# A graph attention kernel on one core: the first block of adj in two transfers, fewer and larger stores, one more small load

## The chip, the cores and the metric

The kernel runs on one core of one Trainium2 chip. The metric is device time in microseconds (us): the median of three runs. The profile is one further execution on the chip, taken by the hardware profiler. Engine names are those of the profile: PE is the matrix engine, PEld its weight load, DVE the vector engine, ACT the scalar engine, POOL GpSimd, SP the engine that here only issues transfers. A small q after a name (SPq) means its sequencer, which waits and issues.

## The reference

One graph attention layer with four heads, a residual and a layer norm. Cut to what matters:

```python
# x: 4096 x 512, adj: 4096 x 4096, W: 512 x 2048, a: 4 x 1024 x 1, all float32
ht  = (x @ W).reshape(N, 4, 512).transpose(1, 0, 2)
src = einsum('hnd,hd->hn', ht, a[:, :512, 0])
dst = einsum('hnd,hd->hn', ht, a[:, 512:, 0])
e   = leaky_relu(src[:, :, None] + dst[:, None, :], 0.01) + adj[None]
h   = einsum('hij,hjd->hid', softmax(e, axis=-1), ht).mean(axis=0)
out = layernorm(x + h)          # over the last axis, eps 1e-5
```

The inputs of adj are mostly zero, with entries up to 1e9 and a diagonal that is not zero. Where the largest entry of a row of adj is far enough ahead of the second, the softmax of that row is one at that column and zero elsewhere.

## The kernel before

The kernel uses that. It finds the column of the largest entry of each row of adj, gathers that row of x, and multiplies it by the mean of the four heads' parts of W; then come the residual and the layer norm. Beside it, it works out a bound on what src and dst can add, and counts the rows in which the lead of the largest entry is too small. If there were any, a general branch (`general`) would do those blocks in full; it is not taken here.

The 4096 rows are 32 blocks of 128, one row on each of the 128 partitions: block `ib` has rows `p * 32 + ib`. A block of adj is 128 x 4096 numbers, 2 MB, and a row of it 16 KB, contiguous in memory. The whole program is written in order by hand (`manual_schedule`), engine by engine.

`leading_rows` does the work. Its loads and its stores are issued on SP, those of `a` on ACT, the gathers on POOL:

- `load_adj` (L124) loads one block of adj into one of six buffers. Blocks 28 to 30 come in two pieces, block 31 in four. `load_x` (L127) and `load_w` (L130) load several blocks of x, or half of W, into one large tile `hold`.
- At the start SP issues adj of block 0, half of W, adj of block 1, the other half of W, adj of blocks 2 to 4, x of blocks 0 to 3. ACT issues the four transfers of `a` (L135), two rows of 2 KB each, into `a_rows`.
- In the loop over blocks `t`, SP loads adj of block `t + 5`. DVE reduces block `t` to maxima of segments (L180), finds the best segment (L187, L189), and POOL gathers that segment (L200). Two blocks behind, DVE finds the column in it (L217, L223) and POOL gathers the row of x (L211). Three blocks behind, PE turns that row (L238), adds x (L246) and multiplies by `w_sum` (L253); ACT takes the statistics (L275, L277) and writes the results over x in `hold` (L286).
- PE also builds `w_sum` from W (L343, from the first half of W on) and, from W and `a`, the vectors for the bound (L353, L359, L367).
- The last blocks are written out by hand after the loop. The results are stored by `store` (L338), all on SP, at the end: blocks 0 to 7 by four, 8 to 15 by two, 16 to 23 by four, then blocks 28 and 29, 24 and 25, 26 and 27, then 30, then 31.

Two kinds of waits hold SP. A transfer into a buffer of adj waits until DVE has read what was in it. And there are eight semaphores for the transfers of SP and ACT together, given out in turn in the order of the program: each transfer waits until the one eight before it has landed. There are 64 such transfers in the program. After the last, SP waits for the semaphores one by one, in a fixed order, and the program ends.

Of the kernel before, what the change touches and what calls it, by code (L numbers as in the profile page):

```python
# [9 lines left out]
F32 = mybir.dt.float32  # L10
# [10 lines left out]
P = 128  # L21
# [9 lines left out]
def gat_resnorm_kernel(  # L31
# [29 lines left out]
    any_bad = keep.tile([1, 1], I32, name="any_bad")  # L61

    leading_rows(tc, x, adj, W, a, out, ident, v, n_bad, any_bad)

    flag = nc.values_load(any_bad[0:1, 0:1], min_val=0, max_val=N)
# [5 lines left out]
def leading_rows(ctx, tc, x, adj, W, a, out, ident, v, n_bad, any_bad):  # L71
# [8 lines left out]
    nc = tc.nc  # L80
    N, D = x.shape
    H = a.shape[0]
    KB, NB = D // P, N // P
    AHEAD = 5
    Q = 4
    PIECES = 4
    LATE = NB - Q
    BEHIND = LATE - Q

    once = ctx.enter_context(tc.tile_pool(name="once", bufs=1))  # L90
    adj_pool = ctx.enter_context(tc.tile_pool(name="adj_pool", bufs=AHEAD + 1))
# [7 lines left out]
    adj_rows = adj.rearrange("(p nb) m -> nb p m", nb=NB)  # L99
# [11 lines left out]
    a_rows = once.tile([2 * H, D], F32, name="a_rows")  # L111

    once.tile([P, 32], F32, name="pad_end")
    adj_t = {}

    def pieces(ib):
        return PIECES if ib == NB - 1 else 2 if ib >= LATE else 1

    def load_adj(ib):
        if 0 <= ib < NB:  # L120
            t = adj_t[ib] = adj_pool.tile([P, N], F32, name="adj_t")
            n = pieces(ib)
            for k in range(n):
                nc.sync.dma_start(t[:, ts(k, N // n)], adj_rows[ib][:, ts(k, N // n)])  # L124
# [4 lines left out]
    def load_w(kb, n):  # L129
        nc.sync.dma_start(hold[:, ds(w_at + kb * H, n * H), :], w_blocks[:, ds(kb * H, n * H), :])  # L130

    load_adj(0)
    for s in range(2):
        for h in range(0, H, H // 2):
            nc.scalar.dma_start(  # L135
                a_rows[ds(s * H + h, H // 2), :], a[ds(h, H // 2), ts(s, D), :].rearrange("h d o -> h (d o)")
            )
    for kb in range(0, KB, 2):
        load_w(kb, 2)
        load_adj(kb // 2 + 1)  # L140
# [196 lines left out]
    def store(queue, lo, n):  # L337
        queue.dma_start(out_rows[:, ds(lo, n), :], hold[:, ds(lo, n), :])  # L338
# [93 lines left out]
    for t in range(NB):  # L432
# [29 lines left out]
        ib = t - PROJECT  # L462
# [25 lines left out]
    for ib in range(BEHIND, LATE):  # L488
        row_norm(ib)
    nc.scalar.activation(xx, xx, AF.Sqrt)  # L490
    for ib in range(0, 2 * Q, Q):
        store(nc.sync, ib, Q)
    for ib in range(2 * Q, 4 * Q, 2):
        store(nc.sync, ib, 2)
    for ib in range(4 * Q, BEHIND, Q):
        store(nc.sync, ib, Q)
    add_x(nc.gpsimd, BEHIND)
    find_column(NB - 2)
# [208 lines left out]
```

## Time and profile before

| | |
|---|---|
| three runs | 234.88, 235.20, 235.32 us; median 235.20 |
| the profiled execution | 234.9 us, of which 233.4 are the span from its first to its last instruction |
| PE, DVE, ACT, POOL busy | 199.9, 191.3, 111.8, 100.7 us |
| DMA | 12257 packets, 97.12 MB, 416 GB/s over the span |
| transfers of SP and ACT (queues q1 and q10) | 88.1 MB; 89.1% of the DMA engines' time over the span |
| gathers of POOL (queue q0) | 8.84 MB; 9.6% |
| a block of adj, from issue to landing | 30.8 us in the median |

The page divides the span into 40 slices of 5.8 us; a digit there is the busy share in tenths. "Chain" is the work that ended last, followed back from the last instruction to what released each step. In a timeline line stand the start, the time taken, the engine, the line of the kernel, the operation, the tiles written and read, and in brackets the idle time before and what ended it. In a line of busy time by stage stand the stage, its length, the busy time of PE, PEld, DVE, ACT and POOL with counts, the granted clock of PE, the DMA engines' busy share and the rate in GB/s.

### The profile page before, as it was taken

The numbers are of one execution on the slowest core, as the hardware profiler recorded it, in microseconds if no ns is written. First come the engines' busy times: TensorE is split into PE (matmuls) and PEld (weight loads), VectorE is DVE, ScalarE is ACT, GpSimd is POOL, SyncE is SP. The second block draws the span as 40 slices with busy tenths as digits, with TensorE's granted clock in tenths as the row PEclk, the third lists the DMA queues.
The fourth block names the chain that finished last, engine by engine and source line by source line (L and its number), as shares of the span: only waits on it lengthen the run. The fifth ranks groups of instructions, "written<-read, shape, count | busy, mean of one in ns | idle before, by whom it ended". The sixth has DMA issues, their size and how long they took to land.

```text
span 233.4 us, 2484 instructions
## 1 busy us (share of the span) xinstructions
PE 199.9 (86%) x683; PEld 105.3 (45%) x683; DVE 191.3 (82%) x300; ACT 111.8 (48%) x267; POOL 100.7 (43%) x215
## 2 busy tenths in 40 slices
PE   0069995999999999999999779879998977999980
PEld 0034644646565555665645244334443433444460
DVE  0548299689929999999788995999999999998881
ACT  2001223014474757575767455545664644188561
POOL 2020234414524464644543452647464564548300
PEclk9999999579999999999999979999999999999997
DMA  6999999999999999999999999999999999999995
GB/s 237 423 432 428 428 438 426 415 439 436 422 421 437 423 431 425 431 419 428 430 430 428 432 423 432 423 430 421 426 433 420 426 423 426 412 424 420 421 414 213
DMA packets 12257, 97.12 MB, mean 416 GB/s; under 512 B 1992, under 2 KB 2440, under 8 KB 6480
## 3 DMA queue, kind: packets, MB, share of 16 engines
q1 hardware_dynamic: 8640, 88.08, 89.1%
q0 software_dynamic: 3584, 8.84, 9.6%
q8 instruction: 6, 0.10, 0.2%
q14 instruction: 11, 0.09, 0.1%
q10 hardware_dynamic: 16, 0.02, 0.0%
HBM read 88.54 MB, written 8.39 MB: 415 GB/s over the span
## 4 chain that ended last, share of the span: by engine, by line
DMA 64%; DVE 21%; PE 11%; SPq 1%; issue 1%; ACT 0%; DVEq 0%
DMA adj_t<-in_adj_dram 53%; DVE seg L180 17%; DMA hold<-in_x_dram 11%; PE o L253 6%; PE o L295 2%; DVE at L189 1%; PE tp L238 1%; DVE top L187 1%; PE o L246 1%; DVE within L223 1%; SPq L130 1%; PE o L291 0%; SPq L124 0%; DVE inner L217 0%; ACT hold L335 0%
## 5 line engine op out<-in xcount | busy, mean ns | idle before, releaser
L180 DVE TENSOR_REDUCE seg<-adj_t 128x128 f32<-128x2048 f32 (+3 forms) x66 | 145.5, 2208 | 28.5 <-DMA adj_t<-in_adj_dram 28.2
L253 PE MATMUL o<-w_sum,yt 128*128 128x512 f32 x248 | 117.6, 616 | 0.7 <-ACT yt L240 0.7
L253 PEld LDWEIGHTS o<-w_sum,yt 128*128 128x128 f32 x248 | 45.6, 196 | 55.2 <-issue 43.9
L240 ACT COPY yt<-tp 128x512 f32<-128x512 f32 x32 | 18.8, 588 | 43.9 <-PE tp L238 43.8
L200 POOL DMA_INDIRECT lead<-in_adj_dram,row x32 | 32.3, 1008 | 14.6 <-POOL row L196 14.6
L211 POOL DMA_INDIRECT y<-in_x_dram,col x32 | 30.9, 964 | 15.4 <-POOL col L225 15.1
L238 PE MATMUL tp<-ident,y 128*128 128x128 f32 x128 | 22.1, 296 | 10.2 <-DMA y<-in_x_dram,col 10.1
L246 PE MATMUL o<-hold,ident 128*128 128x512 f32 x52 | 28.5, 634 | 1.7 <-DMA hold<-in_x_dram 1.7
L343 PE MATMUL o<-hold,ident 128*128 128x512 f32 x32 | 17.3, 696 | 13.6 <-DMA hold<-in_L_gnn_W_dram 13.6
L238 PEld LDWEIGHTS tp<-ident,y 128*128 128x128 f32 x128 | 18.5, 209 | 22.8 <-issue 20.5
L361 ACT COPY wt<-tp 128x512 f32<-128x512 f32 x16 | 9.2, 587 | 38.2 <-PE tp L359 38.2
L196 POOL TENSOR_TENSOR row<-at,first 128x1 uint32<-128x1 uint32 x32 | 6.1, 190 | 43.6 <-DVE at L189 43.6
L367 PEld LDWEIGHTS pv<-at_d,wt 128*128 128x128 f32 x128 | 17.2, 200 | 7.4 <-ACT wt L361 3.7
L260 ACT ACTIVATE sq<-hold 128x512 f32<-128x512 f32 x32 | 19.8, 620 | 0.0
L225 POOL TENSOR_TENSOR col<-start,within 128x1 uint32<-128x1 uint32 x31 | 5.9, 190 | 32.2 <-DVE within L223 32.2
L286 ACT ACTIVATE hold<-o,nm,sd 128x512 f32<-128x512 f32 x24 | 17.2, 771 | 0.0
L277 ACT ACTIVATE sq<-o,nm 128x512 f32<-128x512 f32 x24 | 16.5, 687 | 0.8
L343 PEld LDWEIGHTS o<-hold,ident 128*128 128x128 f32 x32 | 6.9, 225 | 21.5 <-issue 21.5
L367 PE MATMUL pv<-at_d,wt 128*128 128x2 f32 x128 | 16.0, 249 | 0.6 <-ACT wt L361 0.6
L344 ACT ACTIVATE w_sum<-o 128x512 f32<-128x512 f32 x4 | 2.4, 598 | 27.5 <-PE o L343 27.5
L275 ACT ACTIVATE sq<-o 128x512 f32<-128x512 f32 x24 | 14.5, 606 | 0.0
L187 DVE MAX8 top<-seg 128x8 f32<-128x256 f32 (+2 forms) x32 | 11.6, 362 | 1.1
(86 smaller groups left out, 140.0 us busy)
## 6 DMA issues: line engine op xcount, KB each, us to landing
adj_t<-in_adj_dram SPq DMA_DIRECT2D x28, 2048.0 KB, 30.8
adj_t<-in_adj_dram SPq DMA_DIRECT2D x6, 1024.0 KB, 28.1
hold<-in_L_gnn_W_dram SPq DMA_DIRECT2D x2, 2048.0 KB, 16.4
hold<-in_x_dram SPq DMA_DIRECT2D x2, 2048.0 KB, 37.6
out_dram<-hold SPq DMA_DIRECT2D x4, 1024.0 KB, 16.1
out_dram<-hold SPq DMA_DIRECT2D x7, 512.0 KB, 14.4
hold<-in_x_dram SPq DMA_DIRECT2D x3, 1024.0 KB
adj_t<-in_adj_dram SPq DMA_DIRECT2D x4, 512.0 KB, 19.8
```

Of the source, the lines that this page charges most:

```text
L180: nc.vector.tensor_reduce(seg_of[ib][:, ts(k, N // e // n)], adj_t[ib][:, ts(k, N // n)].rearrange("p (s e) -> p s e", e=e), axis=AX.X, op ...
L200: nc.gpsimd.indirect_dma_start(out=lead, out_offset=None, in_=adj_segs[e], in_offset=bass.IndirectOffsetOnAxis(ap=row[:, :1], axis=0),)
L211: nc.gpsimd.indirect_dma_start(out=y, out_offset=None, in_=x, in_offset=bass.IndirectOffsetOnAxis(ap=col[:, :1], axis=0),)
L238: nc.tensor.transpose(tp[:, kb, :], y[:, ds(kb, P, KB)], ident)
L240: nc.scalar.copy(yt, tp)
L246: nc.tensor.matmul(o_ps[ib], ident, hold[:, ib, :], start=start, stop=False)
L253: nc.tensor.matmul(o_ps[ib], yt_of[ib][:, kb, :], w_sum[:, kb, :], start=(start and kb == 0), stop=(kb == KB - 1),)
L260: nc.scalar.activation(sq, hold[:, ib, :], AF.Square, accum_out=xx[:, ib : ib + 1])
L277: nc.scalar.activation(sq, o, AF.Square, bias=nm[:, i], accum_out=sd[:, i])
L286: nc.scalar.activation(hold[:, ib, :], o_ps.pop(ib), AF.Identity, bias=nm[:, i], scale=sd[:, i])
L343: nc.tensor.matmul(o, ident, hold[:, w_at + kb * H + h, :], start=(h == 0), stop=(h == H - 1))
L367: nc.tensor.matmul(pv[:, kb, h : 2 * H : H], wt[:, k, :], at_d[:, k, h : 2 * H : H], start=(k == 0), stop=(k == KB - 1),)
```

## The change

Three edits in `leading_rows`:

1. Adj of block 0 is loaded in two transfers into the same buffer, partitions 0 to 15 and partitions 16 to 127.
2. The eight rows of `a` come in five transfers instead of four: 2, 2, 2, 1 and 1 rows.
3. The results of blocks 8 to 15 are stored by four blocks like their neighbours: two transfers instead of four.

```diff
-    load_adj(0)
-    for s in range(2):
-        for h in range(0, H, H // 2):
-            nc.scalar.dma_start(
-                a_rows[ds(s * H + h, H // 2), :], a[ds(h, H // 2), ts(s, D), :].rearrange("h d o -> h (d o)")
-            )
+    def load_adj_in_parts(ib, *parts):
+        t = adj_t[ib] = adj_pool.tile([P, N], F32, name="adj_t")
+        for lo, hi in zip((0, *parts), (*parts, P)):
+            nc.sync.dma_start(t[lo:hi, :], adj_rows[ib][lo:hi, :])
+
+    load_adj_in_parts(0, P // 8)
+    for s, h, n in ((0, 0, H // 2), (0, H // 2, H // 2), (1, 0, H // 2), (1, 2, 1), (1, 3, 1)):
+        nc.scalar.dma_start(a_rows[ds(s * H + h, n), :], a[ds(h, n), ts(s, D), :].rearrange("h d o -> h (d o)"))
     for kb in range(0, KB, 2):
         load_w(kb, 2)
         load_adj(kb // 2 + 1)
...
     nc.scalar.activation(xx, xx, AF.Sqrt)
-    for ib in range(0, 2 * Q, Q):
-        store(nc.sync, ib, Q)
-    for ib in range(2 * Q, 4 * Q, 2):
-        store(nc.sync, ib, 2)
-    for ib in range(4 * Q, BEHIND, Q):
+    for ib in range(0, BEHIND, Q):
         store(nc.sync, ib, Q)
```

The number of transfers of SP and ACT is 64 after the change as well: one more for adj, one more for `a`, two fewer stores. Here Q is 4, P 128, H 4 and BEHIND 24.

## The prediction

> **What bounds the kernel now.** I read the page first: which resource is never idle.
>
> ```profile
> DMA  6999999999999999999999999999999999999995
> GB/s 237 423 432 428 428 438 426 415 439 436 422 421 437 423 431 425 431 419 428 430 430 428 432 423 432 423 430 421 426 433 420 426 423 426 412 424 420 421 414 213
> DMA packets 12257, 97.12 MB, mean 416 GB/s; under 512 B 1992, under 2 KB 2440, under 8 KB 6480
> DMA 64%; DVE 21%; PE 11%; SPq 1%; issue 1%; ACT 0%; DVEq 0%
> ```
>
> The DMA row is at 9 in every slice but the first and the last, at 412 to 439 GB/s. 97.12 MB at 427 GB/s is 227.4 us of a span of 233.4. So the kernel is one stream of transfers, and about 6 us in which the stream starts and ends. The chain agrees: 64% of it is DMA. To see the two ends I asked for busy time by stage:
>
> ```profile
> 0.00:2.00 2.00, 0.00 (x0) 0.00 (x0) 0.00 (x0) 0.00 (x0) 1.06 (x10) 1.00 0.05 10
> 2.00:2.50 0.50, 0.00 (x0) 0.00 (x0) 0.00 (x0) 0.00 (x0) 0.38 (x6) 1.00 0.60 131
> 2.50:3.00 0.50, 0.00 (x0) 0.00 (x0) 0.00 (x0) 0.42 (x1) 0.00 (x0) 1.00 1.29 360
> 3.00:4.00 1.00, 0.00 (x0) 0.00 (x0) 0.00 (x0) 0.86 (x1) 0.00 (x0) 1.00 0.77 328
> 4.00:9.00 5.00, 0.00 (x0) 0.00 (x0) 0.33 (x1) 0.00 (x0) 0.00 (x0) 1.00 0.99 422
> 24.00:210.00 186.00, 172.94 (x606) 91.77 (x605) 164.61 (x245) 96.97 (x232) 90.32 (x187) 0.96 1.01 427
> 210.00:230.00 20.00, 16.62 (x59) 8.95 (x57) 15.84 (x46) 12.84 (x34) 7.20 (x11) 1.00 1.00 413
> 230.00:231.00 1.00, 0.00 (x0) 0.00 (x0) 0.00 (x0) 0.00 (x0) 0.00 (x0) 0.92 0.73 283
> 231.00:232.00 1.00, 0.00 (x0) 0.00 (x0) 0.00 (x0) 0.00 (x0) 0.00 (x0) 0.50 0.13 49
> ```
>
> The last two figures of a row are the DMA share and GB/s. Nothing flows before 2.0 us. From 2.0 to 4.0 the core moves 0.5 x 131 + 0.5 x 360 + 328 = 574 KB, where full rate gives 854: the ramp costs 280 KB, or 0.66 us. Then the timeline of the first 30 us (start, length, engine and line):
>
> ```profile
> 0.98 0.39 SPq L124 DMA_DIRECT2D adj_t<-in_adj_dram  x1
> 1.06 1.49 ACTq L135 DMA_DIRECT2D a_rows<-in_L_gnn_a_dram  x4
> 8.67 4.48 DVE L180 TENSOR_REDUCE seg<-adj_t 128x128 f32<-128x2048 f32 x2 [8.67 <-DMA adj_t<-in_adj_dram]
> 13.61 6.46 PE L343 MATMUL o<-hold,ident 128*128 128x512 f32 x8 [13.61 <-DMA hold<-in_L_gnn_W_dram]
> 18.34 4.48 DVE L180 TENSOR_REDUCE seg<-adj_t 128x128 f32<-128x2048 f32 x2 [4.20 <-DMA adj_t<-in_adj_dram]
> ```
>
> Block 0 lands at 8.67 and block 1 at 18.34, with half of W between: 4.84 us for each 2 MB. With 16 engines and 8 rows each, a 16 KB row takes 0.605 us. The issue at 0.98 to the landing is 7.69, so starting the stream costs 2.85. What is lost there is not made up: every engine has the same work and is full from there to 230. The tail shifts with it: in the chain, x of the last blocks (issued 176.29, landed 201.51) releases a run of PE work to the last DVE and ACT steps (228.77), the last store and the end.
>
> [...]
>
> **The change, part by part.** The sum is against the profiled execution, 234.9 us (span 233.4 and 1.5 around it), 0.3 under the median of 235.2.
>
> First 16 rows alone. [...]every engine is late by **+1.9**. Below: 0[...]. Above: no more than +1.9[...].
>
> The other 112 rows. [...]I take **+1.0**[...].
>
> The earlier start. A list of 16 rows may be spread over the engines sooner than one of 128. At most the ramp's 0.66 us comes back, at least nothing. The second issue follows within 0.4 us, less than a first row takes, so no engine runs dry. I take **-0.3**.
>
> SP's queue. There is one issue more at the head, 0.39 at most, which pushes W and block 1 back; the landing of rows 0 to 15 is waited for before block 1 is issued, and that of the 112 rows before the second half of W, because eight semaphores go round and each transfer waits for the one eight before. Behind the second wait stand blocks 2 to 4, x and block 5, which stood behind block 0's landing before as well. The cover is data already queued: half of W to 13.6 and block 1 to 18.3. Even a block 0 that lands at 13 leaves 5 us. **0**; without that cover the engines would stand idle until the landing. After the start each transfer waits for the same one as before.
>
> The fifth transfer of a. ACT issues once more, 0.24 to 0.54 us (those of now: 238/309/537 ns), ahead of a table load at 2.58; ACT's first operation that counts is at 20.11, and PE's first use of a at 20.0. On the DMA engines it adds one row's worth of 2 KB: under 0.1. **0**.
>
> Stores of 8 to 15. Two transfers of 1 MB take the place of four of 512 KB. Nothing is computed or waited for longer: blocks 8 to 15 were finished long before SP gets there at 202, and their two transfers wait for the first two quarters of the last block, as the first two did. Blocks 16 to 23 follow two places earlier, so they no longer wait for x; the last stores wait for earlier stores than now. [...]2 MB at the tail's 413 against 427 GB/s is 0.16 us, an estimate with 0 at the other end. **-0.15**. The count of transfers is 64 before and after, so the waits at the end keep their order.
>
> Sum: 1.9 + 1.0 - 0.3 - 0.15 = +2.45, 237.35 against 234.9, and with the 0.3 to the median **237.6**. Ends: 0 + 0 - 0.66 - 0.16 = -0.8 (234.4) and 1.9 + 2.4 - 0 - 0 = +4.3 (239.5).
>
> **Rivals.** *[...]the stream only starts sooner.* Then -0.3 - 0.15 is 234.75, at best 234.4. For it: the ramp is there to be had, and no packet of this trace shows two engines in each other's way. [...]It decides on one point: whether the first 16 rows take under about 1.0 us (0.6 and the gains of 0.45) or more. *Only the first transfer is hit*: 1.9 - 0.45 gives 236.65; for it, nothing shows how 112 rows are laid out[...]. *The 112 rows collide fully*: 239.1 to 239.5. *A wait of SP starves the stream*: for it, SP does wait for landings here; against, over 5 us of queued data; it needs block 0 at 18 us, and each us after that adds 1. *The change isn't what it says*: excluded, the built program holds the two transfers, 16x4096 and 112x4096, on SP.
>
> **How the numbers follow.** [...]in one of three degrees: 0.67, and every degree is slower by more than 0.2%, which is about what a measurement of this kernel can tell from no change (0.47 us: 234.73 to 235.67). [...]0.33. Then the forecast of -0.45 lies at the bound, its spread is 0 to -0.8: 0.21 faster and 0.12 the same. As both signs hold chance, the likeliest case alone is 236.5 to 239.5. The range of 234.4 to 239.3 adds the other case and leaves out the worst collisions and a starved stream.
>
> **What would show it.** Right: DVE's first reduction of block 0 starts at 10.5 to 12.5 instead of 8.67, the first slice of GB/s falls below 237, block 1 is reduced some 2 to 4 us after 18.34, the middle slices stay at 427, and the chain's last steps shift by the same. First transfer alone: the landing of rows 0 to 15, seen where SP issues block 1, comes near 5 us after a start at 2[...]. Wrong: block 0 reduced at 8.3 or earlier, or a later block catching up with its old time, which would mean that the stream has slack that I deny.

## The result, and the profile after

The changed kernel takes 238.18 us (median of four runs, 238.15 to 238.20) against 235.22 for the kernel before: a ratio of 1.0128, 95% interval 1.0111 to 1.0146, or 2.96 us slower. The profiled execution took 238.15 us, with a span of 236.6 (233.4 before). The forecast was 237.6, slower, in a range of 234.4 to 239.3.

The page of the changed kernel, the DMA rows and the chain:

```profile
DMA  6999999999999999999999999999999999999995
GB/s 148 295 432 425 432 433 414 437 434 421 421 427 433 432 426 422 440 417 427 429 426 433 424 431 429 425 429 422 427 433 420 422 427 425 411 426 424 423 397 219
PE 36%; DMA 22%; POOL 18%; issue 17%; DVE 2%; ACT 1%; ACTq 1%; POOLq 0%; DVEq 0%
```

The digits of the DMA row are the same as before; only the rate tells the difference. The first two slices carry 148 and 295 GB/s where they carried 237 and 423: 217 GB/s less over slices of 5.9 us is 1.28 MB, which at 427 GB/s is 3.0 us. From the third slice on the two kernels look alike. So the digit counts time in packets, not bytes: with a digit of 9 the second slice moved 295 GB/s here and 423 before. A packet can take longer: at 5 to 6 us of the stages that follow, a share of 1.15 is 18.4 us of the 16 engines for 19.2 rows of 16 KB, 0.96 us a row, against 0.61 at 4 to 9 us before (0.99 at 422 GB/s). The shares of the chain are of no use here. It runs back through PE, POOL and gathers this time and shows 22% of DMA, though 97.12 MB still fill the span.

Busy time by stage of the changed kernel (the last two figures are the DMA share and GB/s):

```profile
2.00:2.50 0.50, 0.00 (x0) 0.00 (x0) 0.00 (x0) 0.00 (x0) 0.37 (x6) 1.00 2.33 496
2.50:3.00 0.50, 0.00 (x0) 0.00 (x0) 0.00 (x0) 0.18 (x1) 0.00 (x0) 1.00 0.64 98
3.00:4.00 1.00, 0.00 (x0) 0.00 (x0) 0.00 (x0) 1.00 (x1) 0.00 (x0) 1.00 1.30 213
4.00:5.00 1.00, 0.00 (x0) 0.00 (x0) 0.00 (x0) 0.10 (x1) 0.00 (x0) 1.00 0.35 98
5.00:6.00 1.00, 0.00 (x0) 0.00 (x0) 0.00 (x0) 0.00 (x0) 0.00 (x0) 1.00 1.15 315
6.00:7.00 1.00, 0.00 (x0) 0.00 (x0) 0.00 (x0) 0.00 (x0) 0.00 (x0) 1.00 0.82 229
7.00:9.00 2.00, 0.00 (x0) 0.00 (x0) 0.00 (x0) 0.00 (x0) 0.00 (x0) 1.00 1.11 322
9.00:14.00 5.00, 0.00 (x0) 0.00 (x0) 2.01 (x1) 0.00 (x0) 0.00 (x0) 1.00 0.96 342
24.00:210.00 186.00, 173.32 (x603) 92.69 (x602) 164.40 (x241) 94.06 (x225) 88.86 (x186) 0.95 1.01 427
```

A packet is counted in the stage in which it starts, so that a DMA share (the figure before GB/s) can be above 1. From 2.0 to 2.5 the first rows start at 496 GB/s, where the kernel before had 131; the part on the prediction comes back to this. Then comes a hole down to 98 GB/s at 4 to 5 us (SP finds the 16 rows landed at 5.38), and after it 229 to 342 GB/s until 14 us. The middle is at 427 as before.

The timeline of its first 30 us:

```profile
0.97 0.86 SPq L135 DMA_DIRECT2D adj_t<-in_adj_dram  x2
...
2.50 0.35 SPq L124 DMA_DIRECT2D adj_t<-in_adj_dram  x1
...
5.38 0.33 SPq L130 DMA_DIRECT2D hold<-in_L_gnn_W_dram  x1
7.02 5.01 SPq L124 DMA_DIRECT2D adj_t<-in_adj_dram  x3
11.99 4.48 DVE L182 TENSOR_REDUCE seg<-adj_t 128x128 f32<-128x2048 f32 x2 [11.99 <-DMA adj_t<-in_adj_dram]
...
16.84 6.39 PE L345 MATMUL o<-hold,ident 128*128 128x512 f32 x8 [16.84 <-DMA hold<-in_L_gnn_W_dram]
...
21.56 4.48 DVE L182 TENSOR_REDUCE seg<-adj_t 128x128 f32<-128x2048 f32 x2 [4.10 <-DMA adj_t<-in_adj_dram]
```

Block 0 is reduced at 11.99 instead of 8.67 (+3.32), W is used at 16.84 instead of 13.61 (+3.23), block 1 is reduced at 21.56 instead of 18.34 (+3.22). The delay is complete when block 0 has landed, and it stays.

### The profile page after: what moved, and what is told of

It reads as the page before. It is cut to its first block, busy times and chain, and to the rows that moved or that the text cites. A ratio compares the mean times of both kernels' runs of the same rounds, so it can differ in the third digit from the quotient of the medians.

```text
span 236.6 us, 2483 instructions
## 1 busy us (share of the span) xinstructions
PE 200.5 (85%) x683; PEld 106.3 (45%) x683; DVE 190.9 (81%) x300; ACT 111.7 (47%) x267; POOL 100.2 (42%) x215
## 2 busy tenths in 40 slices
DMA packets 11985, 97.12 MB, mean 410 GB/s; under 512 B 1976, under 2 KB 2424, under 8 KB 5952
## 4 chain that ended last, share of the span: by engine, by line
PE 36%; DMA 22%; POOL 18%; issue 17%; DVE 2%; ACT 1%; ACTq 1%; POOLq 0%; DVEq 0%
PE o L255 21%; DMA hold<-in_x_dram 13%; POOL lead L202 6%; POOL y L213 6%; DMA lead<-in_adj_dram,row 5%; PE o L248 5%; PE pv L369 4%; DMA a_rows<-in_L_gnn_a_dram 4%; PE tp L240 3%; POOL sd L283 2%; PE tp L361 2%; PE o L297 1%; POOL row L198 1%; POOL start L209 1%; POOL col L227 1%
## 5 line engine op out<-in xcount | busy, mean ns | idle before, releaser
L255 PEld LDWEIGHTS o<-w_sum,yt 128*128 128x128 f32 x248 | 46.1, 198 | 56.0 <-issue 44.7
L345 PE MATMUL o<-hold,ident 128*128 128x512 f32 x32 | 17.2, 694 | 16.8 <-DMA hold<-in_L_gnn_W_dram 16.8
L248 PE MATMUL o<-hold,ident 128*128 128x512 f32 x52 | 29.4, 652 | 1.4 <-DMA hold<-in_x_dram 1.4
L240 PEld LDWEIGHTS tp<-ident,y 128*128 128x128 f32 x128 | 18.8, 208 | 21.9 <-issue 20.7
```

The costliest lines, as they stand in the source:

```text
L240: nc.tensor.transpose(tp[:, kb, :], y[:, ds(kb, P, KB)], ident)
L248: nc.tensor.matmul(o_ps[ib], ident, hold[:, ib, :], start=start, stop=False)
L255: nc.tensor.matmul(o_ps[ib], yt_of[ib][:, kb, :], w_sum[:, kb, :], start=(start and kb == 0), stop=(kb == KB - 1),)
L345: nc.tensor.matmul(o, ident, hold[:, w_at + kb * H + h, :], start=(h == 0), stop=(h == H - 1))
```

## The experiments

Each was timed beside the kernel before, with 235.17 to 235.22 us for that. "Block 1" is the start of its first reduction in the profiled execution, minus the 18.34 of the kernel before: what the head of the stream lost.

| kernel | median, us | to before | ratio, 95% | block 1 |
|---|---|---|---|---|
| the change | 238.18 | +2.96 | 1.0111 to 1.0146 | +3.22 |
| split alone | 238.36 | +3.19 | 1.0124 to 1.0153 | +3.23 |
| rest alone | 235.58 | +0.41 | 1.0006 to 1.0034 | -0.03 |
| split by columns | 235.34 | +0.17 | 0.9997 to 1.0011 | +0.10 |
| cut at 64 | 240.32 | +5.15 | 1.0215 to 1.0252 | +4.95 |
| cut at 112 | 238.67 | +3.47 | 1.0114 to 1.0161 | +3.16 |
| 16 rows more | 236.72 | +1.54 | 1.0053 to 1.0080 | +1.78 |
| same bytes, 128 partitions | 236.12 | +0.94 | 1.0026 to 1.0054 | +0.69 |
| 112 rows more | 241.41 | +6.23 | 1.0248 to 1.0276 | +6.01 |
| 16 rows, every eighth partition | 236.95 | +1.75 | 1.0051 to 1.0114 | +2.07 |
| 4 rows, partitions 0 to 3 | 236.45 | +1.27 | 1.0037 to 1.0065 | +1.55 |
| 4 rows, partitions 0, 4, 8, 12 | 236.17 | +0.99 | 1.0029 to 1.0057 | +0.87 |
| larger stores alone | 235.31 | +0.11 | 0.9987 to 1.0014 | +0.08 |

"To before" and "block 1" agree within 0.5 us in every row, though the first is of medians and the second of one execution. What these kernels lost before block 1 they lost at the end.

**Which edit.** Theory P is that loading the block by parts of its partitions costs the time. The split alone, with one pair of stores merged so that the count of transfers stays at 64 (lines against the kernel before):

```diff
+    load_adj_in_parts(0, P // 8)
...
+    for ib in range(0, 3 * Q, Q):
+        store(nc.sync, ib, Q)
+    for ib in range(3 * Q, 4 * Q, 2):
+        store(nc.sync, ib, 2)
```

> Adj of block 0 in 16 and 112 partitions; a in four transfers as in the kernel before; of the four small stores only the first two are merged, so that there are still 64 transfers. Theory P[...]: block 0 is reduced at about 12.0 us as in the changed kernel, 237.9 to 238.4 us. Rival T (the tail edits or the fifth load of a cost the time): 235.0 to 236.0 us.

Measured 238.36, block 0 reduced at 12.04: the split is all of it. The rest alone, with the rows of a in six transfers (lines against the changed kernel):

```diff
-    load_adj_in_parts(0, P // 8)
+    load_adj(0)
...
+    for s, h, n in ((0, 0, H // 2), (0, H // 2, H // 2), (1, 0, 1), (1, 1, 1), (1, 2, 1), (1, 3, 1)):
```

> Adj of block 0 in one transfer; stores of 8 to 15 by four; a in six transfers (2, 2, 1, 1, 1, 1 rows) to keep 64. Theory P: block 0 is reduced at 8.7 us, 234.9 to 235.4 us; the larger stores save at most 0.15. Rival T: 237 to 238 us.

235.58, the head unchanged. It lies above the expected 234.9 to 235.4: the other edits save nothing and may cost some tenths. The larger stores alone (62 transfers):

```diff
-    for ib in range(0, 2 * Q, Q):
-        store(nc.sync, ib, Q)
-    for ib in range(2 * Q, 4 * Q, 2):
-        store(nc.sync, ib, 2)
-    for ib in range(4 * Q, BEHIND, Q):
+    for ib in range(0, BEHIND, Q):
```

> The kernel before with the results of 8 to 15 stored by four and nothing else; that leaves 62 transfers. Theory L (1 MB stores queued ahead make the last gather of a segment late and with it the end): as with the rest alone, 235.4 to 235.7 us, DVE idle before L219 for 0.5 us or more, block 1 at 18.3. Rival A (the six transfers of a cost what the rest alone cost): 235.0 to 235.3 us and no wait of DVE there.

235.31, no difference that can be told, with runs from 235.05 to 236.73. DVE did wait 1.0 us at L217, but in an execution at 236.73, which is 1.4 above the median. The cut by columns, next, has the same stores: its DVE waits 0.7 us there in an execution at 235.43, beside a median of 235.34. So the wait of theory L comes about, but not its cost. Whether the 0.41 of the rest alone is the six transfers of a or chance is open.

**The second transfer, or its shape?** The same number of transfers, the same 256 KB first, but cut by columns (against the changed kernel):

```diff
-            nc.sync.dma_start(t[lo:hi, :], adj_rows[ib][lo:hi, :])
+            nc.sync.dma_start(t[:, lo * N // P : hi * N // P], adj_rows[ib][:, lo * N // P : hi * N // P])
```

> The changed kernel, with adj of block 0 split by columns: 512 of each of the 128 partitions first (256 KB, as many bytes as the 16 rows), then the other 3584. Theory P: [...]the loss is gone: block 0 reduced at 8.4 to 9.0 us, 234.8 to 235.5 us. Rival S (a second transfer at the head, or what SP waits for because of it, costs the time, whatever its shape): 237.5 to 238.3 us.

235.34 us, and the loss is gone (block 0 at 8.82, block 1 at 18.44):

```profile
18.44 4.48 DVE L182 TENSOR_REDUCE seg<-adj_t 128x128 f32<-128x2048 f32 x2 [4.15 <-DMA adj_t<-in_adj_dram]
```

Neither the second issue nor the new waits of SP cost anything that can be told (0.17); the cut by partitions does. This also rules out the starved stream. Then the cut at partition 64 (`P // 2`):

> The changed kernel, with the cut at partition 64. Theory P[...]: [...]each runs at half rate, 2 x 2.4 us more; block 0 reduced at about 13.5 us, 239.5 to 240.1 us. Rival S: the same as the cut at 16, 238.2. Rival K (only a transfer of few rows is slow[...]): less than the cut at 16, 235.2 to 236.5 us.

Timeline of that kernel, and two of its stages:

```profile
14.05 4.48 DVE L182 TENSOR_REDUCE seg<-adj_t 128x128 f32<-128x2048 f32 x2 [14.05 <-DMA adj_t<-in_adj_dram]
23.29 4.48 DVE L182 TENSOR_REDUCE seg<-adj_t 128x128 f32<-128x2048 f32 x2 [3.77 <-DMA adj_t<-in_adj_dram]
```

```profile
7.00:9.00 2.00, 0.00 (x0) 0.00 (x0) 0.00 (x0) 0.00 (x0) 0.00 (x0) 1.00 1.14 248
9.00:12.00 3.00, 0.00 (x0) 0.00 (x0) 0.00 (x0) 0.00 (x0) 0.00 (x0) 1.00 0.94 192
```

The core moves 192 to 248 GB/s where it moved 414 to 437 before, and a row of 16 KB takes 1.2 to 1.3 us of an engine (from the share and the rate), twice the 0.61 of the full stream. Block 1 is 4.95 late. Two halves at half rate would be 2 x 2.42 = 4.84 late, an estimate from the 4.84 us of 2 MB. Block 0 (14.05) and the time (240.32) lie a little above what was expected. That a transfer has few rows is not the cause here: each has 64.

**The two terms by themselves.** One load more ahead of block 0, into a part of hold that x overwrites later; its data is not used. In these loads, and in the three of this kind further on, the first pair of small stores is merged, as in the split alone.

```diff
+    nc.sync.dma_start(hold[0:16, 0:8, :].rearrange("p b d -> p (b d)"), adj_rows[1][0:16, :])
     load_adj(0)
```

> The kernel before (first pair of small stores merged, to keep 64 transfers) with one more load ahead of block 0: 16 rows of 16 KB into partitions 0 to 15 of a part of hold that x overwrites later; the data is not used. At full rate 256 KB are 0.6 us. Theory P: [...]block 0 reduced at 10.7 to 11.2, 237.2 to 237.7 us. Rival K2 (the 112 rows alone are the trouble): 235.4 to 235.9 us.

> The control: as the extra load of 16 rows, but the same 256 KB as 512 columns of all 128 partitions. Theory P: its bytes at full rate, 0.6 to 0.7 us: block 0 reduced at 9.3, 235.7 to 236.0 us. If a further transfer costs by itself, as much as the 16 rows.

> The kernel before (first pair of small stores merged) with one more load ahead of block 0: 112 rows of 16 KB into partitions 16 to 127 of hold, not used, overwritten later. At full rate 1.79 MB are 4.26 us, which gives 239.3 to 239.6. Theory P[...]:[...] 240.5 to 241.9 us.[...]

The second of these fills `hold[:, 0, :]` from 512 columns of all partitions, the third partitions 16 to 127. Busy time by stage, first the 16 rows, then the wide load:

```profile
3.00:4.00 1.00, 0.00 (x0) 0.00 (x0) 0.00 (x0) 0.80 (x1) 0.00 (x0) 1.00 1.21 180
4.00:5.00 1.00, 0.00 (x0) 0.00 (x0) 0.00 (x0) 0.00 (x0) 0.00 (x0) 1.00 0.30 66
5.00:6.00 1.00, 0.00 (x0) 0.00 (x0) 0.00 (x0) 0.00 (x0) 0.00 (x0) 1.00 1.17 496
```

```profile
3.00:4.00 1.00, 0.00 (x0) 0.00 (x0) 0.00 (x0) 0.82 (x1) 0.00 (x0) 1.00 0.95 289
4.00:5.00 1.00, 0.00 (x0) 0.00 (x0) 0.00 (x0) 0.00 (x0) 0.00 (x0) 1.00 0.93 397
```

The hole at 4 to 5 us is there again (66 GB/s), and absent with the same bytes spread wide (397). The 16 rows land 4.5 us after their issue, the wide load 3.3. The wide load shifts block 1 by 0.69, about its bytes at full rate (its 236.12 us is 0.1 above what was expected). The 16 rows shift it by 1.78: less than expected (236.72 us, where 237.2 was the least), and 1.2 above the 0.6 of full rate. The 112 rows shift it by 6.01 where full rate is 112/128 of 4.84 us, 4.24: 1.8 above it, and the 241.41 us are inside theory P's 240.5 to 241.9. Together 1.2 + 1.8 = 3.0, against the 3.22 of the change.

**Which partitions, or few rows?** Partitions 0, 8, 16 to 120 instead of 0 to 15:

> As the extra load of 16 rows, the same 256 KB[...], but into partitions 0, 8, 16 to 120.[...] Theory P:[...] 0.6 to 1.2 us earlier than that run: block 1 reduced at 18.9 to 19.5 (20.12 with partitions 0 to 15, 19.03 with the wide load), 235.6 to 236.2 us. Rival K[...]: block 1 at 20.1, 236.7 us.

Block 1 at 20.41, no better: the expectation is missed, and the runs scatter from 236.28 to 239.10. But the two transfers are not alike in their issue, as the timeline of SP shows, first every eighth partition, then 0 to 15:

```profile
0.97 0.63 SPq L132 DMA_DIRECT2D hold<-in_adj_dram  x1
1.66 0.56 SPq L124 DMA_DIRECT2D adj_t<-in_adj_dram  x1
```

```profile
0.97 0.40 SPq L132 DMA_DIRECT2D hold<-in_adj_dram  x1
1.43 0.41 SPq L124 DMA_DIRECT2D adj_t<-in_adj_dram  x1
```

The strided list took 0.63 to issue, and the core moved 107 GB/s at 2.0 to 2.5 us where the other moved 434. A later start may cover what the choice of partitions saved, so this run decides nothing. Four rows make a cleaner pair: the same rows, into partitions 0 to 3 or 0, 4, 8 and 12.

```diff
+    nc.sync.dma_start(hold[0:4, 0:8, :].rearrange("p b d -> p (b d)"), adj_rows[1][0:4, :])
```

> As the extra load of 16 rows, but four rows of 16 KB (64 KB) into partitions 0 to 3.[...] Theory P:[...] 64 KB cost nearly as much as 256 KB: block 1 reduced at 20.0 to 20.8, 236.6 to 237.3 us.[...] Full rate: 18.9 to 19.1, 235.7 to 236.1 us.

> The same four rows into partitions 0, 4, 8 and 12[...]. Theory P: one row at full rate, 0.6 us, and up to 0.3 more if a strided list is issued more slowly: block 1 at 18.9 to 19.3, 235.6 to 236.2 us. Rival K: as with partitions 0 to 3.

Stages with the rows in partitions 0 to 3, then in 0, 4, 8 and 12:

```profile
2.00:3.00 1.00, 0.00 (x0) 0.00 (x0) 0.00 (x0) 0.49 (x1) 0.38 (x6) 1.00 1.25 197
3.00:4.00 1.00, 0.00 (x0) 0.00 (x0) 0.00 (x0) 0.80 (x1) 0.00 (x0) 1.00 0.56 86
4.00:5.00 1.00, 0.00 (x0) 0.00 (x0) 0.00 (x0) 0.00 (x0) 0.00 (x0) 1.00 0.60 231
```

```profile
2.00:3.00 1.00, 0.00 (x0) 0.00 (x0) 0.00 (x0) 0.30 (x1) 0.37 (x6) 1.00 0.60 131
3.00:4.00 1.00, 0.00 (x0) 0.00 (x0) 0.00 (x0) 0.98 (x1) 0.00 (x0) 1.00 0.76 217
4.00:5.00 1.00, 0.00 (x0) 0.00 (x0) 0.00 (x0) 0.00 (x0) 0.00 (x0) 1.00 0.93 393
```

64 KB into partitions 0 to 3 shift block 1 by 1.55, nearly as much as 256 KB into 0 to 15 (1.78), if a little less than expected (19.89 and 236.45 us, where 20.0 and 236.6 were the least). Into 0, 4, 8 and 12 they shift it by 0.87, as expected, though that list took 0.78 to issue instead of 0.38 and its stream started later. Rival K, that only the small number of rows makes a transfer slow, asked for no difference. The difference shows in the stages: 86 and 231 GB/s against 217 and 393, with the later start on the side of the higher rate. The two medians, 236.45 and 236.17, lie close, and their intervals overlap; the pair rests on the stages of one execution each.

One rival was not tested. In every run the rows that are read change together with the partitions that are written: partition p takes row 32p or 32p + 1 of adj. So no run alone excludes that the reading of these rows is slow. The extra loads don't settle it: their rows lie 512 KB apart in memory for partitions in a row, 2 MB for 0, 4, 8 and 12, which was the quicker of its pair, and 4 MB for every eighth, which was slower than expected. So the cut by partitions is shown as the cause; how it acts, no run shows.

**The order of the parts** (`P - P // 8`):

> The changed kernel with the cut at partition 112: 112 rows first, then the last 16. Theory P[...]: block 1 reduced at 20.7 to 21.4, 237.3 to 238.0 us. If the two parts cost the same in either order: block 1 at 21.6, 238.2 us.

Block 1 at 21.50, so the two parts cost about the same in either order (238.67 us; the intervals overlap), and theory P's 20.7 to 21.4, which was my estimate, lay 0.1 to 0.8 us lower. Why the 112 rows are slow is not shown by any run.

No run beat the kernel before, and none points to a version that would.

## Why the prediction was right

**The bound and the place: right.** This stream, with a digit of 9 in every slice but the first and the last, gave back nothing of what its start lost: block 1 late by 3.22, the span longer by 3.2.

**The first 16 rows: right in kind, too large in size.** I took +1.9, my estimate, which no trace of the kernel before shows, with -0.3 for the earlier start beside it, so +1.6 net. The load by itself showed 1.2 net. The sign that I had named came: rows 0 to 15 landed at 5.38, near 5, though SP waited with W for them and not with block 1.

**The 112 rows: right in kind, too small.** I took +1.0, with 0 and 2.4 as its ends, my estimate again, which no trace shows. The load by itself showed 1.8. These two errors, -0.4 and +0.8, cancel in part; that the total came within 0.6 us owes something to luck. The upper end of each, 1.9 and 2.4, held.

**The earlier start: not shown.** The first half microsecond moved 496 GB/s instead of 131, but the length of the list did not decide it. In the cut at 112, with 112 rows first, it moved 528, and in larger stores alone, with the 128 rows of the kernel before, 360:

```profile
2.00:2.50 0.50, 0.00 (x0) 0.00 (x0) 0.00 (x0) 0.00 (x0) 0.37 (x6) 1.00 1.59 360
```

With 360 instead of 131 block 1 was still reduced at 18.42, against 18.34. So there was no sign of a gain to be had, and none in the cut by columns (+0.10).

**SP's queue: cost right, reasoning wrong in a detail.** I said that block 1 would wait for rows 0 to 15 and the second half of W for the other 112. The timeline shows block 1 issued at 2.50, held by nothing that lands late, the second half of W at 5.38 on the landing of rows 0 to 15, and blocks 2 to 4 from 7.02 on, held by the rows of a. The first transfer of a stands ahead of adj in the round of semaphores, and I had counted it after. It cost nothing, since W's first half ran to 16.84; the cut by columns has waits at the same places, and took 0.17 us more.

**The tail: the -0.15 is not there.** Larger stores alone: +0.11, inside the noise; the rest alone: +0.41. So no run shows that fewer and larger stores save time. And the last steps do not shift by the same, as I had said they would. DVE in the tail of the changed kernel:

```profile
219.67 0.84 DVE L219 MAX8 inner<-lead 128x8 f32<-128x32 f32 x7
221.22 0.23 DVE L219 MAX8 inner<-lead 128x8 f32<-128x64 f32 x1 [0.72 <-DMA lead<-in_adj_dram,row]
```

Before, these eight ran as one group at 216.53 without a wait. Now the last of them waits 0.72 us for the gather of the last block. The last ACT step starts at 232.33 instead of 228.21, 4.1 later, but from there to the end of the span it takes 4.3 instead of 5.2 us. So the end is 3.2 later all the same. In the cut by columns the last ACT step starts at 229.80, 1.6 later than before, and the kernel takes 0.17 more. So in these runs it is not this step that sets the end; what shortens the finish, no run isolates.

**The rivals.** A stream that only starts sooner: fallen, by the split alone (+3.19) and the cut at 64 (+5.15). Only the first transfer hit (236.65): fallen, by the 112 rows alone. The 112 rows at their worst (239.1 to 239.5): 238.2 stays under it. A starved stream: fallen, by the cut by columns.

## What to carry to other kernels

Where a load fills all 128 partitions, try a cut by columns before one by partitions: the cut by columns cost 0.17 us here, the cut at partition 16 cost 3.2, the cut at 64 cost 5.2, for the same two megabytes. In a kernel whose DMA row is at 9 from end to end, look at the rate and not at the digit (a 9 stood for 295 GB/s here and for 423 before), and price each edit at the head of the stream as if it were at the end. A transfer of few rows was not cheap for being small: 64 KB on partitions 0 to 3 made block 1 1.55 us late, 256 KB over all partitions 0.69.

## What the runs showed of the hardware

Rows of 16 KB took longer beside a load into part of the partitions, and not only those of that load. With four rows into partitions 0 to 3, the whole core fell to 86 GB/s at 3 to 4 us. In that stage the share of 0.56 is 9.0 us of 16 engines, and 86 GB/s are 5.2 rows of 16 KB: 1.7 us a row in the mean, against 0.61 on the full stream. At 2 to 3 us 197 KB had started, three times the 64 KB of the load, which was issued first (0.98 us, block 0 at 1.41); so the slow rows were, as I estimate from these figures, for the most part those of block 0. With the four rows in partitions 0, 4, 8 and 12 it was 0.92. What held the rows up is not shown.

The two lists with a stride in their partitions took longer to issue: 0.63 us for 16 rows and 0.78 for four, against 0.40 and 0.38 without, in one execution each. The stream behind them started later: 107 GB/s instead of 434 at 2.0 to 2.5 us, and 131 instead of 197 at 2 to 3. That the stride is the reason is not shown, since the two lists of 64 consecutive rows took 0.57 and 0.58.
